# Second cross attention of a perceiver block: probabilities transposed in 32 by 32 blocks and moved by DMAs and copies, context in two buffers, and a planner with measured overlaps

## The chip, the cores and the metric

The kernel runs on one core of one Trainium2 chip. A core has a matrix engine (TensorE, "PE" in the profile), a vector engine (VectorE, "DVE"), a scalar engine (ScalarE, "ACT"), a general-purpose engine (GpSimd, "POOL") and a sync engine (SyncE, "SP") that here only issues DMAs. Each works through its own list of instructions in order and waits on semaphores for the others. Data lies in an on-chip memory with 128 partitions (rows); matrix products land in a separate accumulator memory of eight banks. All arithmetic is in 32-bit floats. The metric is the device time of one execution in microseconds (us), given as the median of several runs.

## The reference

There are 32 sequences of 64 tokens with 256 features (x), each with 256 context tokens of 256 features. Six layers follow one another, each added to x:

```
x = x + L0_xattn(ctx, layernorm(x))      # cross attention, 16 heads of 64, keys: context and latents
x = x + L0_attn(layernorm(x))            # linear attention, 16 heads of 16
x = x + L0_ffn(layernorm(x))             # gated feed-forward, hidden 768
x = x + L1_xattn(layernorm(x), ctx, ctx, mask)   # cross attention, 16 heads of 16
x = x + L1_attn(layernorm(x))            # recurrent layer (sLSTM), 64 units
x = x + L1_ffn(layernorm(x))             # 8 experts, entmax gates
```

The layer that the change is about is `L1_xattn`, standard cross attention: with q = x Wq + bq, k = ctx Wk + bk, v = ctx Wv + bv, split in 16 heads of 16,

```
p   = softmax(q k^T / 4 + mask)          # 64 queries by 256 context tokens, per head
out = (p v) Wo + bo
```

## The kernel before

The 2048 tokens are 16 tiles of 128 rows (two sequences each). The kernel has three parts that overlap at their seams:
- the first phase: `L0_xattn`, one sequence b after the other (32 of them);
- the second phase: the next three layers and the recurrent one, in 8 groups of two tiles (`linear_attention`, `feed_forward`, `queries`, then per tile `keys_values`, `scores`, `weighted`, `projected`, and `slstm_router` at the end of a group);
- the experts: gates, gathers of token rows, two matrix products per expert, and accumulating stores.

The order of the work is not the order of the program text. A planner (`Plan`) records every operation with what it reads and writes, a rank, and an estimated length (`PlanEngine.length`), and then lists all of them greedily: of the operations that are ready it takes the one that can start first by its own clock, ties by rank, at most 12 ranks ahead of the oldest operation left. So a change in an estimated length can reorder every engine's list. All recorded operations carry the line of the one helper that issues them (L375 in the profile), so the profile's groups are told apart by tile names. Tiles lie at fixed places of one large buffer, the arena (`ar.put(phase, tag, size, places)`); places may overlap those of an earlier part, and then wait for its last use. An operation written as `pl.copy` or `pl.either` may go to ACT or to DVE, as the planner finds.

In the first phase the softmax probabilities are transposed without PE: DVE transposes 32 by 32 blocks (`pl.vector.transpose` into tile `bT`), and 16 block moves put the blocks where they belong in `pT`: four on POOL, four on ACT or DVE, eight as DMAs on SP's queue. The planner takes 0.65 us to issue a DMA. 

In the second cross attention a run is one tile t with one half c of the heads, 32 runs in all. `scores` makes eight score products (tile `xsc`, four banks), masks each on DVE with its minimum (`tensor_tensor_reduce` into `xne` and `xnm`; a custom DVE operation in the profile), and takes the exponential on ACT into `xpr` with its sum into `xsm`. `weighted` then transposes the unnormalised probabilities on PE (16 transposes of 128 by 128 into the tile `xpTp`, four to a bank), copies each bank to `xpT`, transposes the reciprocal sums (`xrT`), multiplies values by the transposed probabilities (`xpo`), scales with the reciprocals and adds the two head halves and the value bias `vb` into `oT`. `projected` multiplies by `x_wo` (`xpw`) and adds to x.

Of the kernel before, what the change touches and what calls it, by code (L numbers as in the profile page):

```python
# [14 lines left out]
P = 128  # L15
# [139 lines left out]
class Slots:  # L155
# [7 lines left out]

    def take(self, t_):
        self.free.sort()
        self.next += 1
        return self.free.pop(0)
# [5 lines left out]
class Area:  # L173
# [9 lines left out]
    def room(self, t_, k):  # L183
# [3 lines left out]
        return all(a.next == len(a.asked) and a.live[j] is None for a, j in self.rivals[i])  # L187

# [21 lines left out]
class Plan:  # L210
# [10 lines left out]
    HOP = 0.06  # L221

    def __init__(self, tc):
        self.tc, self.ops, self.slots, self.news = tc, [], {}, []
        self.rank, self.group, self.lane, self.last = 0.0, None, None, {}
# [24 lines left out]
    @contextmanager  # L250
    def together(self, length):

        assert self.group is None
        self.group = []
        yield
        calls, self.group = self.group, None
        self.add({"PE": (length, calls)})
# [41 lines left out]
    def run(self, ahead):  # L299
# [7 lines left out]
        while todo:  # L307
# [3 lines left out]
            for op in sorted(ready, key=lambda op: op.rank):  # L311
# [5 lines left out]
                if op.news and not self.has_room(op):  # L317
                    if "PE" in op.ways and (short is None or op.rank < short.rank) and self.has_room(op, True):
                        short = op
                    continue  # L320
                for engine, (length, _) in op.ways.items():
                    at = free[engine]
                    for other in op.before:
                        at = max(at, other.end if other.on == engine and other.end == other.done else other.done + self.HOP)
                    for t_ in op.uses:
                        at = max(at, t_.free_at)
                    key = at, op.rank
# [9 lines left out]
            op.end = op.done = free[engine] = at + length  # L337
# [12 lines left out]
    def has_room(self, op, later=False):  # L350
# [10 lines left out]
        return True  # L361

# [76 lines left out]
class PlanEngine:  # L439
# [34 lines left out]
    def length(engine, name, args, kw):  # L474
# [10 lines left out]
        if name == "memset":  # L485
            return 0.1 + 0.5e-3 * n
        if engine == "ACT":
            if isinstance(kw.get("scale"), View):
                return 0.6
            return (0.12 + 0.91e-3 * n if name == "copy" else 0.33 + 0.66e-3 * n) + (0.19 if "accum_out" in kw else 0)  # L490
        if engine == "DVE":
            return 0.15 + 1.04e-3 * n + (0.08 if name == "tensor_tensor_reduce" else 0)
        if engine == "POOL":
            return 0.7 if n < 64 else 0.3 + 2.0e-3 * n
# [4 lines left out]
def kernel(ctx: ExitStack, tc: tile.TileContext, d: dict, out: bass.AP):  # L499
# [130 lines left out]
    with ExitStack() as sa:  # L630
# [21 lines left out]
        ar.put(1, "cx", 1024, 14336, 15360)  # L652
# [9 lines left out]
        for tag, size, *at in (  # L662
# [6 lines left out]
            ("ffh", 1536, 17920, 19456), ("sg", 512, 20992, 21504),  # L669
            ("xn0x", 256, 16384), ("xn1x", 256, 16640), ("xTx", 512, 16896, 17408), ("xq", 1024, 32256, 33280),  # L670
            ("xcT", 1024, 22016, 23040), ("xkT", 1024, 24064, 25088), ("xv", 1024, 30208, 31232),
            ("xpr", 2048, 26112, 28160), ("xpT", 512, 35328, 35840, 36352, 36864), ("xne", 256, 37376, 37632, 37888),
# [101 lines left out]
        def l0_context(t):  # L774

            pl.rank = 2 * t - 6.0
            cx = ar.tile([P, 4, D], F32, tag="cx", name=f"cx{t}")
            for b2 in range(2):
                b = 2 * t + b2
                pl.sync.dma_start(  # L780
                    out=cx[:, 2 * b2 : 2 * b2 + 2, :],
                    in_=d["ctx"][b * S2 : (b + 1) * S2, :].rearrange("(t p) d -> p t d", p=P),
# [14 lines left out]
            srcs = [cx[:, i, :] for i in range(4)]  # L797
            norm(srcs, srcs, f"c{t}", "c")
            affine(cx, 0, 4)
# [1134 lines left out]
```

## Time and profile before

| what | value |
|---|---|
| median of 3 runs | 1634.33 us (1632.51 to 1634.55) |
| profiled execution | 1633.02 us, its span 1631.3 us |
| mean granted clock of TensorE | 0.991 |
| instructions | 25951 |
| PE busy | 1579.4 us, 97% of the span |
| DVE busy | 1088.2 us, 67% |
| ACT busy | 693.8 us, 43% |
| POOL busy | 422.1 us, 26% |
| DMA | 95.02 MB, 58 GB/s over the span |

A span is the time from the first to the last instruction; the execution is a little longer. An engine's busy time counts each instant once, also where two of its instructions overlap, but the busy time of a group of instructions may overlap that of another group. Matmul instructions overlap their neighbours, and a matmul of 32-bit floats appears as two records. PEld is the loading of weights into the array, which runs beside the matmuls. Idle time of an engine is put down to the engine or transfer that ended it.

### The profile page before, as it was taken

How to read it: one execution, taken by the hardware profiler on the slowest of the kernel's cores; microseconds unless marked ns; L12 is line 12 of the kernel's file. 1: busy time of each engine (PE TensorE's matmuls, PEld its weight loads, DVE VectorE, ACT ScalarE, POOL GpSimd, SP SyncE). 2: the span in 40 equal slices, each digit the busy share in tenths (PEclk: the TensorE clock that was granted, in tenths of full speed). 3: DMA queues.
4: the chain of work that ended last, by engine and by line, in shares of the span. 5: the costliest groups of instructions: out<-in, count | busy, mean ns of one | idle time of the engine just before them, and what ended most of it. 6: DMA issues, size and time to landing. Idle time of an engine off the chain costs nothing. (4 is left out here: it accounts for less than half of the span.)

```text
span 1631.3 us, 25951 instructions
## 1 busy us (share of the span) xinstructions
PE 1579.4 (97%) x9226; PEld 1106.8 (68%) x9226; DVE 1088.2 (67%) x3089; ACT 693.8 (43%) x1813; POOL 422.1 (26%) x524
## 2 busy tenths in 40 slices
PE   8999999999999999999989999999999999999996
PEld 6556656565665656666556777777777776878885
DVE  6657666676766757776755788888888788762230
ACT  4434344353533535334421454454544547432332
POOL 5123123230333223331311221221212112223342
PEclk9999999999999999999999999999999999999998
DMA  6112112121112211122121000010000220455391
GB/s 212 38 30 59 38 31 44 38 59 29 39 30 46 47 34 40 30 71 53 38 54 49 14 27 27 18 37 14 27 27 20 85 80 19 133 144 141 69 307 31
DMA packets 95601, 95.02 MB, mean 58 GB/s; under 512 B 9327, under 2 KB 85936, under 8 KB 95472
## 3 DMA queue, kind: packets, MB, share of 16 engines
q1 hardware_dynamic: 89952, 85.41, 19.2%
q0 software_dynamic: 5520, 7.94, 2.4%
q8 instruction: 74, 1.21, 0.3%
q14 instruction: 55, 0.45, 0.1%
HBM read 63.63 MB, written 7.47 MB: 44 GB/s over the span
## 5 line engine op out<-in xcount | busy, mean ns | idle before, releaser
L375 PE MATMUL pu<-arena 128*128 128x512 f32 (+1 forms) x768 | 301.0, 615 | 3.5 <-ACT arena L375 2.8
L375 PE MATMUL sc<-arena 128*128 128x320 f32 x1024 | 290.5, 436 | 0.0
L375 PEld LDWEIGHTS sc<-arena 128*128 128x128 f32 x1024 | 190.8, 190 | 95.3 <-issue 19.2
L375 ACT ACTIVATE arena<-sc,nmax 128x320 f32<-128x320 f32 x256 | 134.4, 527 | 250.3 <-DVE nmax L375 241.8
L375 PEld LDWEIGHTS pu<-arena 128*128 128x128 f32 (+1 forms) x768 | 113.9, 189 | 175.9 <-issue 159.1
L375 POOL COPY arena<-arena 32x640 f32<-32x640 f32 (+1 forms) x161 | 108.9, 676 | 404.1 <-DVE arena L375 300.4
L375 DVE TENSOR_REDUCE nmax<-sc 128x1 f32<-128x320 f32 x256 | 121.8, 484 | 105.5 <-PE sc L375 104.1
L375 POOL TENSOR_TENSOR arena<-arena 128x1024 f32<-128x1024 f32 (+3 forms) x72 | 118.5, 1646 | 166.6 <-DVE arena L375 109.7
L375 ACT ACTIVATE arena<-arena,xnm 128x256 f32<-128x256 f32 x256 | 127.1, 500 | 52.1 <-DVE xnm L375 51.9
L375 DVE COPY arena<-pu 128x512 f32<-128x512 f32 x62 | 42.7, 689 | 115.4 <-PE pu L375 115.2
L375 DVE CUSTOM_DVE_ANT_0 arena<-xsc,arena 128x256 f32<-128x256 f32 x256 | 101.2, 421 | 17.7 <-ACT arena L375 10.3
L375 DVE TENSOR_TENSOR arena<-arena,sm 128x1280 f32<-128x1280 f32 x64 | 108.1, 1690 | 2.2
L375 DVE STREAM_TRANSPOSE arena<-arena 128x512 f32<-128x512 f32 (+1 forms) x192 | 104.4, 594 | 3.6
L375 ACT COPY arena<-pu 128x512 f32<-128x512 f32 x66 | 38.4, 585 | 128.0 <-PE pu L375 128.0
L375 POOL DMA_INDIRECT out<-arena x25 | 39.6, 1585 | 102.8 <-DVE arena L375 71.2
L375 PE MATMUL pqk<-arena 64*128 64x256 f32 x512 | 63.1, 383 | 1.6 <-ACT arena L375 1.6
L375 PE MATMUL xpTp<-ident,arena 128*128 128x128 f32 x512 | 63.6, 274 | 0.9 <-ACT arena L375 0.9
L375 PE MATMUL xak<-arena 128*128 128x512 f32 x128 | 62.3, 610 | 0.0
L375 PEld LDWEIGHTS xpTp<-ident,arena 128*128 128x128 f32 x512 | 56.9, 141 | 7.2 <-DVE arena L375 2.2
L375 PE MATMUL xav<-arena 128*128 128x256 f32 x256 | 61.5, 384 | 0.0
L375 PEld LDWEIGHTS po<-arena 128*64 128x64 f32 x1024 | 55.5, 137 | 8.8 <-issue 8.3
L375 PE MATMUL mepha<-arena 128*128 128x256 f32 x256 | 60.1, 385 | 1.4 <-ACT arena L375 1.4
(395 smaller groups left out, 2800.9 us busy)
## 6 DMA issues: line engine op xcount, KB each, us to landing
arena<-in_m_w SPq DMA_DIRECT2D x26, 1024.0 KB
arena<-arena SPq DMA_DIRECT2D x256, 80.0 KB
arena<-in_ctx SPq DMA_DIRECT2D x32, 256.0 KB
arena<-in_ctxT SPq DMA_DIRECT2D x16, 512.0 KB
x<-in_x SPq DMA_DIRECT2D x16, 128.0 KB
arena<-in_l0x_wkv SPq DMA_DIRECT2D x2, 1024.0 KB
arena<-arena SPq DMA_DIRECT2D x16, 128.0 KB
out<-x SPq DMA_DIRECT2D x16, 128.0 KB
```

Of the source, the lines that this page charges most:

```text
L375: r = getattr(real, name)(*[get(a) for a in args], **{k: get(a) for k, a in kw.items()})
```

## The change

The change has five parts.

First, the second cross attention no longer transposes on PE. DVE transposes the exponentials of each sequence of the run in 32 by 32 blocks (one instruction over 128 rows by 1024 columns, two per run) into a tile `xbT`, and 16 moves of 32 rows by 512 columns bring them to `xpT`: four on POOL, four on ACT, eight as DMAs of 64 KB on SP's queue. `xpr` now has three buffers of half the size; `xbT` and `xpT` have one each. A copy to POOL, to ACT or a DMA is chosen by a function `move`, which the first phase uses too.

Second, the value bias no longer enters each run. It is multiplied by `x_wo` once, ahead of the groups, and added to the row `x_bo`; the sum of the two head halves, now without the bias, goes to POOL. Four steps of the recurrent layer go from DVE to POOL in all groups but the last.

Third, the first phase's context tile `cx` is two tiles of one sequence each, so each is loaded, scaled and released by itself.

Fourth, the places in the arena change: the hidden layer of the feed-forward (`ffh`) has one buffer instead of two, and its second place now holds the second buffer of the context load `xcT`, which the second expert's weights will later overlie.

Fifth, the planner's estimates change: PE groups are taken 1.5% shorter, an engine is free again 0.085 us (DVE), 0.11 (ACT) or 0.05 (POOL) before its instruction ends, lengths for ACT, DVE and POOL are new, and the start of an operation counts when its buffer comes free.

```diff
+    def when(self, k):
+        return sorted(self.free)[k]
...
+    OVERLAP = {"DVE": 0.085, "ACT": 0.11, "POOL": 0.05}
...
-        self.add({"PE": (length, calls)})
+        self.add({"PE": (0.985 * length, calls)})
...
+                since = self.since(op)
                 for engine, (length, _) in op.ways.items():
-                    at = free[engine]
+                    at = max(free[engine], since)
                     for other in op.before:
-                        at = max(at, other.end if other.on == engine and other.end == other.done else other.done + self.HOP)
+                        at = max(at, other.done + (0.03 if other.on == engine else self.HOP))
...
-            op.end = op.done = free[engine] = at + length
+            op.end = op.done = at + length
+            free[engine] = op.end - self.OVERLAP.get(engine, 0.0)
...
-            return (0.12 + 0.91e-3 * n if name == "copy" else 0.33 + 0.66e-3 * n) + (0.19 if "accum_out" in kw else 0)
+            return (0.12 + 0.91e-3 * n if name == "copy" else min(0.33 + 0.66e-3 * n, 0.6)) + (0.09 if "accum_out" in kw else 0)
         if engine == "DVE":
-            return 0.15 + 1.04e-3 * n + (0.08 if name == "tensor_tensor_reduce" else 0)
+            return 0.15 + 1.04e-3 * n + (0.02 if name == "tensor_tensor_reduce" else 0)
         if engine == "POOL":
-            return 0.7 if n < 64 else 0.3 + 2.0e-3 * n
+            if n < 64:
+                return 0.7 if n <= 2 else 1.0
+            return 0.15 + 0.97e-3 * n if name == "tensor_copy" else 0.3 + 1.9e-3 * n
...
-        ar.put(1, "cx", 1024, 14336, 15360)
+        ar.put(1, "cx", 512, *range(14336, 16384, 512))
...
-            ("ffh", 1536, 17920, 19456), ("sg", 512, 20992, 21504),
+            ("ffh", 1536, 17920), ("sg", 512, 20992, 21504),
...
-            ("xcT", 1024, 22016, 23040), ("xkT", 1024, 24064, 25088), ("xv", 1024, 30208, 31232),
-            ("xpr", 2048, 26112, 28160), ("xpT", 512, 35328, 35840, 36352, 36864), ("xne", 256, 37376, 37632, 37888),
+            ("xcT", 1024, 22016, 19456), ("xkT", 1024, 23040, 24064), ("xv", 1024, 30208, 31232),
+            ("xpr", 1024, 25088, 26112, 27136), ("xbT", 2048, 28160), ("xpT", 2048, 35328), ("xne", 256, 37376, 37632, 37888),
...
+        def move(n, o, i, tight=False):
+            if n == 0:
+                pl.gpsimd.tensor_copy(o, i)
+            elif n == 1 and tight:
+                pl.scalar.copy(o, i)
+            elif n == 1:
+                pl.copy(o, i)
+            else:
+                pl.sync.dma_start(out=o, in_=i)
...
+        pl.vector.tensor_copy(vd, vb.unsqueeze(2).to_broadcast([P, 2, P]))
+        pvb = bank([P, D], "pvb")
+        with pl.together(0.9):
+            for c in range(2):
+                mm(pvb, vd[:, c], x_wo[:, c, :], start=(c == 0), stop=(c == 1))
+        pl.vector.tensor_tensor(row("x_bo"), pvb, row("x_bo"), ALU.add)
...
+            bT = ar.tile([P, 4, 2, 2, 4, B_], F32, tag="xbT", name=f"xbT{nm}")
+            for b2 in range(2):
+                pr = ar.tile([P, 4, S2], F32, tag="xpr", name=f"xpr{nm}_{b2}")
+                for j in range(4):
                     ne = ar.tile([P, S2], F32, tag="xne", name=f"xne{nm}_{j}_{b2}")
                     nmax = sp.tile([P, 1], F32, tag="xnm", name=f"xnm{nm}_{j}_{b2}")
                     pl.vector.tensor_tensor_reduce(ne, scs[j][:, b2, :], mb, 1.0, 3.0e38, ALU.add, ALU.min, nmax)
-                    pl.scalar.activation(
-                        pr[:, b2, j, :], ne, AF.Exp, bias=nmax, scale=-1.0, accum_out=sm[:, b2, j : j + 1]
+                    pl.scalar.activation(pr[:, j, :], ne, AF.Exp, bias=nmax, scale=-1.0, accum_out=sm[:, b2, j : j + 1])
+                pl.vector.transpose(
+                    bT[:, :, b2].rearrange("p k d j c -> p j d k c"),
+                    pr.rearrange("p j (d k c) -> p j d k c", d=2, c=B_),
+                )
+            pT = ar.tile([P, 4, 2, 2, 4, B_], F32, tag="xpT", name=f"xpT{nm}")
+            for n in range(4):
+                for a in range(4):
+                    k = (a + n) % 4
+                    move(
+                        n,
+                        pT[B_ * k : B_ * k + B_, a].rearrange("p b d j c -> p (b d j c)"),
+                        bT[B_ * a : B_ * a + B_, k].rearrange("p b d j c -> p (b d j c)"),
+                        tight=True,
                     )
...
-            pTs = {}
-            for b2 in range(2):
-                for kc in range(2):
-                    pT = ar.tile([P, 4, P], F32, tag="xpT", name=f"xpT{nm}_{b2}_{kc}")
-                    pT_ps = bank([P, 4, P], f"xpTp{nm}_{b2}_{kc}")
-                    with pl.together(T4):
-                        for j in range(4):
-                            tr(pT_ps[:, j, :], pr[:, b2, j, kc * P : (kc + 1) * P], ident)
-                    pl.copy(pT, pT_ps)
-                    pTs[b2, kc] = pT
...
-                                pTs[b2, kc][:, j, :],
+                                pT[:, :, b2, kc, j, :],
...
-            pl.vector.scalar_tensor_tensor(
-                oT[:, c], om[:, :, 0, :], vb[:, c : c + 1], om[:, :, 1, :], ALU.add, ALU.add
-            )
+            pl.gpsimd.tensor_tensor(oT[:, c], om[:, :, 0, :], om[:, :, 1, :], ALU.add)
...
-            pl.vector.tensor_scalar(il[:, :, :, 1:], il[:, :, :, 1:], 20.0, None, ALU.min)
+            side = pl.vector if g == NG - 1 else pl.gpsimd
+            side.tensor_scalar(il[:, :, :, 1:], il[:, :, :, 1:], 20.0, None, ALU.min)
...
-            pl.vector.tensor_tensor(tmp, m[:, :, 0:S], lf[:, :, 1:], ALU.add)
-            pl.vector.tensor_tensor(tmp, tmp, m[:, :, 1:], ALU.subtract)
+            side.tensor_tensor(tmp, m[:, :, 0:S], lf[:, :, 1:], ALU.add)
+            side.tensor_tensor(tmp, tmp, m[:, :, 1:], ALU.subtract)
...
-            pl.vector.tensor_tensor(iz[:, :, 1:], tmp2, z, ALU.mult)
+            side.tensor_tensor(iz[:, :, 1:], tmp2, z, ALU.mult)
```

## The prediction

> **What bounds the kernel now.** First I read the page's busy shares (columns: busy time, share of the span, instructions), then its 40 slices:
>
> ```profile
> PE 1579.4 (97%) x9226; PEld 1106.8 (68%) x9226; DVE 1088.2 (67%) x3089; ACT 693.8 (43%) x1813; POOL 422.1 (26%) x524
> ...
> PE   8999999999999999999989999999999999999996
> ...
> DVE  6657666676766757776755788888888788762230
> ```
>
> TensorE (PE) is full from end to end; VectorE (DVE) comes nearest in slices 23 to 34. That share is an average, so next the windows (length, then busy time and instructions of each engine, clock, DMA share, GB/s): the second phase's steady part, the first phase, the passage between them, the experts.
>
> ```profile
> 905.30:1364.80 459.50, 451.06 (x3454) 337.96 (x3453) 371.70 (x1365) 234.72 (x680) 86.01 (x160) 1.00 0.10 34
> 100.00:750.00 650.00, 647.80 (x3126) 409.20 (x3125) 441.87 (x857) 276.68 (x668) 182.19 (x182) 1.00 0.19 41
> 840.00:870.00 30.00, 24.13 (x150) 14.47 (x147) 21.92 (x68) 7.28 (x14) 9.28 (x16) 0.89 0.14 29
> 1400.00:1632.00 232.00, 209.20 (x1217) 182.29 (x1215) 78.47 (x355) 70.02 (x180) 75.32 (x67) 0.96 0.48 136
> ```
>
> PE idles 0.3% of the first phase and 8.4 of 459.5 us in the second: matmul time taken out of either shortens the run until another engine is late. The period of a group comes from the tile view of the query projection (count; shortest, median, longest; first and last start):
>
> ```profile
> L375 PE MATMUL xaq<-arena x64: 379/379/379, 905.3 to 1364.8; 128*128 128x256 f32 x64
> ```
>
> Eight groups start in it, so a group is (1364.8 - 905.3) / 7 = 65.6 us. By the window above it holds DVE 371.7 / 7 = 53.1 us (81%), ScalarE (ACT) 33.5, GpSimd (POOL) 12.3, and PE idle 1.2.
>
> **What is removed.** The groups by form (count | busy, mean ns of one | idle before, releasers):
>
> ```profile
> L375 PE MATMUL xpTp<-ident,arena 128*128 128x128 f32 x512 | 63.6, 274 | 0.9 <-ACT arena L375 0.9
> L375 DVE COPY arena<-xpTp 128x512 f32<-128x512 f32 x60 | 40.0, 685 | 4.5 <-PE xpTp L375 4.3
> L375 ACT COPY arena<-xpTp 128x512 f32<-128x512 f32 x68 | 38.6, 587 | 39.9 <-PE xpTp L375 39.8
> L375 DVE STREAM_TRANSPOSE arena<-arena 128x512 f32<-128x512 f32 x128 | 83.5, 690 | 3.6
> L375 DVE STREAM_TRANSPOSE arena<-arena 128x256 f32<-128x256 f32 x64 | 25.8, 402 | 0.0
> ```
>
> Matmuls overlap, so 63.6 us counts overlaps twice. What a transpose takes from the path is its pace, from PE's timeline (start, length, instruction):
>
> ```profile
> 921.70 1.91 PE L375 MATMUL xpTp<-ident,arena 128*128 128x128 f32 x16
> 923.45 0.38 PE L375 MATMUL xrT<-ident,arena 128*128 128x128 f32 x2
> ```
>
> (923.45 - 921.70) / 16 = 0.109 us; times 512 = **56.0 us** off PE, 7.0 per group. Ends of this term: 55 and 63.6.
>
> **What is added, and where it lies.** Per group of four runs (two token tiles by two channel halves), each run now having two DVE transposes of 128x1024 and 16 block moves of 32x512:
> - DVE: by the two transpose rows an element costs (690 - 402) / 256 = 1.125 ns, so 128x1024 is 690 + 512 x 1.125 = 1266 ns; 8 of them are 10.1. The instruction order of the changed kernel has, per group, fewer: 8 PSUM copies (5.5), 2 copies of xrT (0.8), 4 additions of oT now on POOL (1.4), 4 steps of the recurrent layer moved to POOL (1.3), one each of laq and xak (1.2); more: one copy of tr_me, one normalisation (1.1). Net +1.0: DVE 54.2 us.
> - ACT: 16 block copies; 32x640 took 722 ns, so 32x512 about 0.58: +9.2, less 8.5 x 0.587 = 5.0, plus about 1 taken over from DVE: 38.8.
> - POOL: 16 block copies at 0.61 (766 ns x 4/5) are 9.8, four oT additions 2.2, the recurrent steps about 2.4: 26.7. POOL's own order also carries the small powers of the layer norms behind block copies that wait for DVE.
> - SP: 8 DMAs of 64 KB per run; the first phase does the same with 80 KB.
>
> At PE's new period of 65.6 - 7.0 = 58.6 us DVE stands at 92%, ACT at 66%, POOL at 46%: all below PE, DVE barely. That cover pays for the added work; gone, each us of DVE is a us per group.
>
> **The new wait.** The context matmuls (xpo) wait for all 16 moves, and behind them on PE stands everything else. The moves wait on SP for DVE's transposes and, the target having one buffer, for the previous xpo; behind them on SP queue the next context load and, once a group, the stores of x. The delay is bounded by the first phase's last use of the same path (timelines of DVE, SP, PE):
>
> ```profile
> 845.87 1.63 DVE L375 STREAM_TRANSPOSE arena<-arena 128x512 f32<-128x512 f32 x3
> ...
> 847.20 5.16 SPq L375 DMA_DIRECT2D arena<-arena  x8
> ...
> 854.03 2.38 PE L375 MATMUL pu<-arena 128*128 128x512 f32 x5
> ```
>
> Eight issues take 5.2 us, and all had landed 6.8 us after the first. Softmax of a run (scores done 1064.3, last exponential done about 1069.0) takes 4.7 us when DVE does nothing else; in the order of the changed kernel about 2.2 us of other DVE work stands between (two additions to x, layer-norm statistics, a masked product). Scores to ready: 4.7 + 2.2 + 1.3 + 6.8 = 15.0 us at most. In the changed order PE has between a run's scores and its xpo, at the paces of the rows, 21 us for half of the runs and 13.9 for one of the short ones (projections of the feed-forward layer 5.2, keys and values 3.5, attention of the first kind 1.9, other scores 1.1, the rest 2.2). So a short run may wait 0 to 1.1 us: 16 x that is **0 to 18 us**. I take **5**, near the low end, since the first phase leaves 13.6 us between scores and context and PE lost nothing there:
>
> ```profile
> 506.67 1.34 PE L375 MATMUL sc<-arena 128*128 128x320 f32 x4
> ...
> 521.60 9.35 PE L375 MATMUL pu<-arena 128*128 128x512 f32 x24
> ```
>
> **Two rules against the change.** The Trainium skill, "VectorE: DVE Perf Modes", section "Rules for kernel authors", sends a 128x128 transpose to TensorE where PSUM will do as destination; by it the trade saves nothing, and the sum would stay at 1633. The rows say otherwise here, because PE, not DVE, is full. The Trainium skill, "DMA: Bandwidth & Descriptors", section "Anatomy of one DMA", gives a DMA about 2.0 us fixed plus its bytes over 436 GB/s; an estimate from it, were eight served one by one, is 17 us per run, 10 more than the trace's bound, and 16 short runs would make the sum about 1740. The trace's eight overlap.
>
> **The small edits.** The value bias folded into x_bo adds two matmul calls and one copy ahead of the loop: +0.9 (xpw's two calls pace 0.9). The second-phase chain gets longer by POOL's 555 ns in place of DVE's 329 (four times a group); PE's feed-forward and key work covers it, else 1 us per group. The layer-0 context in two tiles turns 32 POOL operations of 2526 ns into 64 of 1351, +5.6 us on an engine 28% busy there: 0, covered by PE's own work; uncovered it is those 5.6. One feed-forward buffer instead of two: its users are a group apart, 0. The second expert's weights now lie over the second context buffer and can load only after its last use; if that is late, 2 MB at the 236 to 369 GB/s of the first 20 us cost 6 to 9 us. The planner's new durations reorder all queues. Its reach is the idle time elsewhere: 11 us in the first 100, 5.9 at the passage (with the clock at 0.89), 22.8 at the end, 12 of them after the last matmul. I take 0 with ends of -15 and +10: in the first phase the changed order leaves about the same PE work between scores and context, and no row tells the sign.
>
> **The sum**, against the profiled execution (1633.0; span 1631.3): 1633.0 - 56.0 + 0.9 + 5 + 0 = 1582.9. The median shown is 1.3 higher: **1584 us**, 3.1% less.
>
> **Rivals.**
> 1. *DVE sets the pace* (0.20). For: 92% with in-order waits, where the fullest 100 us of the trace (1300 to 1400) had it at 83.7%. Against: its instructions start 0.08 us before the previous one ends when work is queued, so a denser stream needs less than its sum. At 88% a group takes 54.2 / 0.88 = 61.6: 4.0 x 8 = 32 saved, 1603 us; range 1597 to 1625.
> 2. *The new order also fills idle time* (0.10): 10 to 15 of the 40 us named above: 1570.
> 3. *SP holds the moves* (0.07, the slower side). Once a group two output stores stand in the queue before eight moves, and wait for DVE's last x; in the trace SP stood 224.5 us for that in 8 waits, the longest 46.5, with nothing urgent behind. Each us that x comes after the moves' inputs stops xpo and PE. Break-even is 55.1 / 8 = 6.9 us a group; at 10 us it is +25: 1659. Against: the stores are placed where their inputs are planned to be ready.
> 4. *The transposes were hidden* (0.03): DVE keeps most of its idle 12.5 us a group, and nothing comes of it: 1634. Against: PE's 1.2 us idle in a group.
>
> **How the numbers follow.** The forecast has 0.60 with 1569 to 1597 of its own. 0.2% (3 us) is about what this kernel's times can tell apart. Faster: 0.60 + 0.20 + 0.10 = 0.90; same 0.03; slower 0.07. The range 1562 to 1610 leaves out the slower rival, the unchanged one, the upper half of the first rival's, and some of the second's: about 0.2.
>
> **What the profile after should show.** No xpTp; start of the second phase unmoved (first xaq near 905); the group period 58.6 to 60; DVE at 90% or more there; PE's waits on DMA or DVE before xpo under 10 us; 64 DVE transposes near 1.27 us. A period of 61 or more with PE waiting for DVE is rival 1; SP waiting for DVE x with PE waiting for moves is rival 3. I am wrong if the idle time at the passage or in the experts moves by over 15 us.

## The result, and the profile after

The changed kernel takes 1658.6 us (median; 1657.0 to 1661.6), the kernel before 1633.9 in the same session: a ratio of 1.0155 with a 95% interval of 1.0137 to 1.0172. It is slower by 1.5%; the forecast was 1584, faster by 3%. The profiled execution took 1661.6 us, span 1659.8.

First the page of after, busy shares and three of the rows of 40 slices:

```profile
PE 1546.5 (93%) x8718; PEld 1066.8 (64%) x8718; DVE 1058.1 (64%) x3004; ACT 747.6 (45%) x1904; POOL 542.7 (33%) x744
...
PE   7999999999999999999989988989889798899996
...
DVE  7656666666666756667555688778787778643131
...
PEclk9999999999999999999989999999999896999998
```

PE's busy time fell by 33 us, not by the 55 of the forecast, and its idle time rose from 52 to 113. The digits say where: from slice 21 on, which is the passage and the second phase. The windows of after (columns as before: length, busy time of PE, PEld, DVE, ACT, POOL, then clock, DMA share, GB/s) put numbers on the second phase's steady part, the first phase, the passage and the experts:

```profile
909.00:1376.90 467.90, 417.92 (x2978) 299.74 (x2977) 361.09 (x1271) 275.53 (x736) 175.59 (x317) 0.95 0.22 59
100.00:750.00 650.00, 644.15 (x3107) 407.08 (x3107) 421.46 (x848) 276.31 (x673) 192.97 (x206) 1.00 0.19 40
840.00:870.00 30.00, 21.82 (x80) 10.71 (x76) 17.30 (x54) 6.02 (x13) 8.13 (x11) 0.83 0.13 27
```

The query projections mark the groups (first and last start):

```profile
L395 PE MATMUL xaq<-arena x64: 379/379/793, 909.0 to 1376.9; 128*128 128x256 f32 x64
```

So I divide the span in three: head (to the first query projection), seven groups, and end (from the last query projection). Before: 905.3, 459.5, 266.5. After: 909.0, 467.9, 282.9. The group went from 65.6 to 467.9 / 7 = 66.8 us, where the forecast had 58.6; PE idles 50.0 of the 467.9 us (8.4 before), and the clock granted in this stretch is 0.95 (1.00 before).

A seventh of this stretch is a rough measure of a group, because the planner puts work of the first group ahead of the first query projection and work of the last one behind the last. In before the first of the seven intervals is 53.4 us and the other six are 67.4 to 67.6. So the windows from the second to the seventh query projection, five whole groups, stand beside it; first before, then after:

```profile
958.68:1295.72 337.04, 332.11 (x2562) 248.02 (x2561) 275.39 (x991) 168.56 (x491) 67.05 (x128) 1.00 0.09 31
965.09:1303.85 338.76, 304.79 (x2241) 218.70 (x2240) 267.84 (x940) 201.00 (x540) 135.33 (x247) 0.96 0.23 62
```

By these "inner" groups PE has 512 records a group before and 448 after; a group took 337.04 / 5 = 67.4 us and takes 67.8, and the forecast's 7.0 less would be 60.4. Either way a group is some 7 to 8 us longer than forecast.

What PE waits for there (instruction, releaser; total, times, longest):

```profile
PE tr_ff L395 <- DVE arena L395: 8.0, 5, 2.0
PE xrT L395 <- POOL arena L395: 6.3, 12, 0.7
PE tr_la L395 <- ACT arena L395: 5.0, 5, 1.2
PE ffg L395 <- DVE xnm L395: 3.7, 1, 3.7
PE tr_xa L395 <- DVE arena L395: 3.2, 6, 1.2
PE xpo L395 <- ACT arena L395: 3.0, 2, 2.2
PE xpo L395 <- DVE xnm L395: 3.0, 2, 1.8
```

Many small waits, most of 0.5 to 2 us, on the layer norms (tr_...), on GpSimd (xrT) and ahead of the context matmuls, where the moves end (xpo). Summed over the whole view, 33.9 us end with VectorE, 9.1 with ScalarE, 6.3 with GpSimd and 0.6 with a DMA; 9.8 of all these stand before xpo. No single one explains the loss. PE's timeline at the end of one group (start, length, instruction, idle before):

```profile
1104.95 0.66 PE L395 MATMUL tr_la<-ident,arena 128*128 128x128 f32 x4 [1.17 <-ACT arena L395]
1107.10 1.09 PE L395 MATMUL tr_ff<-ident,arena 128*128 128x128 f32 x4 [1.49 <-DVE arena L395]
1108.11 2.09 PE L395 MATMUL xsc<-arena 32*128 32x256 f32 x16
1110.13 3.49 PE L395 MATMUL ffg<-arena 128*128 128x256 f32 x8
1113.45 1.89 PE L395 MATMUL laq<-arena 128*128 128x256 f32 x8
```

After two idles the scores take 2.09 us (1.15 elsewhere) and the first gate projection 3.49 (1.89 elsewhere): the clock is granted at half here. The trace records such a stretch of 6.8 us at this place in four groups running, and 92 us in all against 20 in before (each without the stretch that ends the trace).

The second thing to see lies on VectorE. Of its groups by form, in three steady groups of each kernel (count | busy, mean ns | idle), first before, then after:

```profile
L375 DVE SCALAR_TENSOR_TENSOR x<-arena,r_lay,x 128x256 f32<-128x256 f32 x6 | 2.6, 482 | 0.1
L375 DVE TENSOR_SCALAR arena<-x,mv_ff,r_ff 128x256 f32<-128x256 f32 x3 | 1.2, 409 | 0.0
L375 DVE SCALAR_TENSOR_TENSOR r_xa<-t_xa,r_xa 128x2 f32<-128x2 f32 x3 | 0.5, 153 | 0.0
```

```profile
L395 DVE SCALAR_TENSOR_TENSOR x<-arena,r_lay,x 128x256 f32<-128x256 f32 x6 | 5.7, 985 | 0.1
L395 DVE TENSOR_SCALAR arena<-x,mv_ff,r_ff 128x256 f32<-128x256 f32 x3 | 2.9, 966 | 0.0
L395 DVE SCALAR_TENSOR_TENSOR r_xa<-t_xa,r_xa 128x2 f32<-128x2 f32 x3 | 1.7, 566 | 0.0
```

The same instructions take two to four times as long. The timelines of DVE and of POOL at one such place:

```profile
1161.62 0.57 DVE L395 SCALAR_TENSOR_TENSOR r_xa<-t_xa,r_xa 128x2 f32<-128x2 f32 x1
1162.27 0.56 DVE L395 SCALAR_TENSOR_TENSOR nmr_xa<-mv_xa,r_xa 128x2 f32<-128x2 f32 x1
...
1166.27 1.89 DVE L395 SCALAR_TENSOR_TENSOR x<-arena,r_lay,x 128x256 f32<-128x256 f32 x2
```

```profile
1161.34 2.95 POOL L395 COPY arena<-arena 32x512 f32<-32x512 f32 x4 [3.75 <-DVE ve_lay L395]
...
1166.29 1.59 POOL L395 TENSOR_TENSOR x<-x,rows 128x256 f32<-128x256 f32 x2
```

Each long one lies beside a GpSimd instruction: the first two beside the block copies, the third beside an addition. Summed over the second phase (909 to 1377), the excess over the usual length of the same form is some 20 us in after (19.8 by my reckoning) and a few us in before (2.4; up to 7 by other choices of the usual length). Instructions that read PSUM, the accumulator memory, show none of it (the softmax's maximum is 0.41 us beside GpSimd and 0.41 alone), nor do the transposes (1.24 and 1.24), nor the layer norms' statistics, which read one operand of SBUF, the on-chip memory (0.43 and 0.41). The Trainium skill, "GPSIMD Engine Reference", section "Specifications", says that GpSimd's memory interfaces are shared with VectorE and contend with its instructions that have two SBUF inputs or run in a two-port mode: the rows with two SBUF inputs agree, and I had not looked for it. Of the tensor_scalar, which has one such input beside two pointers to scalars and is stretched too (409 to 966 ns), no run here shows the mode.

### The profile page after: what moved, and what is told of

It reads as the page before. It is cut to its first block, busy times and chain, and to the rows that moved or that the text cites. A ratio compares the mean times of both kernels' runs of the same rounds, so it can differ in the third digit from the quotient of the medians.

```text
span 1659.8 us, 25703 instructions
## 1 busy us (share of the span) xinstructions
PE 1546.5 (93%) x8718; PEld 1066.8 (64%) x8718; DVE 1058.1 (64%) x3004; ACT 747.6 (45%) x1904; POOL 542.7 (33%) x744
## 3 DMA queue, kind: packets, MB, share of 16 engines
q8 instruction: 70, 1.15, 0.3%
## 5 line engine op out<-in xcount | busy, mean ns | idle before, releaser
L395 POOL COPY arena<-arena 32x640 f32<-32x640 f32 (+2 forms) x289 | 204.0, 706 | 563.8 <-DVE arena L395 414.4
L395 PE MATMUL pu<-arena 128*128 128x512 f32 (+1 forms) x768 | 305.3, 615 | 4.5 <-DMA arena<-arena 2.9
L395 POOL TENSOR_TENSOR arena<-arena 128x512 f32<-128x512 f32 (+2 forms) x157 | 141.9, 923 | 162.3 <-DVE arena L395 123.2
L395 DVE STREAM_TRANSPOSE arena<-arena 128x512 f32<-128x512 f32 (+2 forms) x256 | 182.9, 753 | 6.5 <-ACT arena L395 4.7
L395 ACT COPY arena<-arena 32x512 f32<-32x512 f32 (+1 forms) x192 | 125.1, 651 | 58.2 <-DVE arena L395 46.9
L395 DVE TENSOR_TENSOR arena<-arena,sm 128x1280 f32<-128x1280 f32 x64 | 101.3, 1583 | 1.9
L395 POOL DMA_INDIRECT out<-arena x25 | 39.8, 1592 | 101.6 <-DVE arena L395 81.3
L395 PE MATMUL po<-arena 128*64 128x128 f32 x1024 | 61.3, 275 | 2.7 <-DVE arena L395 2.4
L395 PE MATMUL xav<-arena 128*128 128x256 f32 x256 | 63.8, 394 | 0.0
L395 PE MATMUL xak<-arena 128*128 128x512 f32 x128 | 62.4, 613 | 1.4 <-DVE x L395 1.4
L395 PE MATMUL pw<-arena 128*128 128x256 f32 x256 | 59.8, 386 | 0.0
```

The source lines that it names most:

```text
L395: r = getattr(real, name)(*[get(a) for a in args], **{k: get(a) for k, a in kw.items()})
```

## The experiments

The theories. **Moves:** xpo waits for the 16 moves. **GpSimd:** its new work stretches VectorE's instructions, and its own queue is later. **VectorE:** a backlog of its load in its in-order queue; over a steady group it is busy for 53.7 of 67 us, but unevenly, as the windows of its two halves show below. **Order:** the planner's new durations and overlaps give an order without slack. **Clock:** short idles set off half-clock stretches. All ratios are to the kernel before in the same session. "Period" is a seventh of the time from first to last query projection, "inner" the mean of the five intervals from the second to the seventh, "end" what follows the last, and "half clock" the time in us at half the clock, without the stretch that ends the trace. Where period and inner differ, the first or the last interval is short or long (over all runs single intervals go from 48.8 to 74.3 us), and inner is the better measure.

```profile
1139.00:1174.00 35.00, 30.79 (x228) 22.22 (x228) 31.71 (x127) 21.32 (x60) 14.30 (x22) 1.00 0.26 71
1104.00:1139.00 35.00, 31.16 (x225) 22.26 (x225) 23.93 (x73) 20.77 (x55) 13.73 (x29) 0.90 0.18 46
```

VectorE (the third busy time, behind PE and PEld) has 31.7 of 35 us in one half and 23.9 in the other, in which the clock is at 0.90.

| run | ratio (95% interval) | period | inner | end | half clock |
|---|---|---|---|---|---|
| before | 1 | 65.6 | 67.4 | 266.5 | 20 |
| after | 1.0155 (1.0137 to 1.0172) | 66.8 | 67.8 | 282.9 | 92 |
| old_planner | 1.0256 (1.0225 to 1.0287) | 63.9 | 66.1 | 299.7 | 130 |
| new_planner_alone | 1.0122 (1.0103 to 1.0140) | 67.6 | 69.7 | 263.6 | 10 |
| fill_pe | 1.0145 (1.0126 to 1.0164) | 65.4 | 65.8 | 280.8 | 61 |
| free_context | 1.0273 (1.0250 to 1.0296) | 65.4 | 66.0 | - | - |
| pool_cut | one run, 1631.0 us | 62.9 | 63.0 | - | - |
| moves_on_act | 1.0057 (1.0034 to 1.0079) | 63.1 | 66.0 | 288.9 | 51 |
| lean_to_act | 1.0027 (1.0014 to 1.0041) | 61.5 | 63.9 | 287.4 | 41 |
| half_blocks | 1.0048 (1.0034 to 1.0062) | 64.8 | 66.5 | 274.7 | 38 |
| planner_knows | 1.0065 (1.0039 to 1.0091) | 61.8 | 63.5 | 293.0 | 65 |
| both_reliefs | 0.9987 (0.9978 to 0.9997) | 61.9 | 63.8 | 281.4 | 41 |
| both_last_on_pe | 0.9987 (0.9973 to 1.0001) | 62.1 | 63.7 | 280.3 | 44 |
| reliefs_planner_knows | 1.0133 (1.0116 to 1.0150) | 63.2 | 64.7 | 295.2 | 68 |
| relief_side | 1.0008 (0.9995 to 1.0021) | 63.0 | 64.4 | 285.2 | 55 |
| relief_lean_more | 1.0028 (1.0016 to 1.0040) | 61.1 | 63.9 | 293.9 | 38 |
| relief_free_context | one run, 1652.7 us | 62.1 | 63.7 | - | - |
| relief_slack | 0.9948 (0.9928 to 0.9968) | 58.6 | 61.4 | 300.8 | 55 |
| after_slack | 1.0001 (0.9987 to 1.0015) | 62.4 | 62.3 | 284.4 | 79 |
| slack_last_on_pe | 0.9870 (0.9853 to 0.9886) | 59.3 | 62.0 | 286.5 | 41 |

One caution holds for most of them. Only free_context, fill_pe, pool_cut and relief_free_context keep the order of the kernel that they start from. In all others the planner makes a new order, and a new order alone can be worth 20 to 25 us (new_planner_alone below, and reliefs_planner_knows against both_reliefs), so in those runs the edit and the new order aren't parted.

### Body and planner apart

old_planner has the new body and the planner class of before; new_planner_alone the reverse.

> The changed kernel's body (transposes on VectorE, block moves, everything else) under the planner of before: its durations, no overlaps, no 0.985. If the planner's new, tighter durations are what lost the time (an order without slack, in which PE arrives at each result just before it is there), this takes 1585 to 1605 us, faster than before by 2 to 3%, and PE idles under 2.5 us a group. If the body itself loses (moves, longer chains through DVE and POOL), it stays at 1640 to 1670 with PE idle of 5 us or more a group.

> The body of before under the planner of after. If the planner's durations lose the time, PE idles more than the 52 us of before and the time rises to 1645 to 1660 us. If the body loses, it stays within 1620 to 1640.

Measured: each half alone is slower than before, by 2.6 and 1.2%. With the old body, the new planner's group is 67.6 us in place of 65.6 (inner 69.7 in place of 67.4), and VectorE's stretching some 15 us in place of a few: the new order alone sets VectorE's work beside GpSimd's. The new body under the old planner has a shorter group (63.9, inner 66.1), but loses 17 us in the head and 33 at the end. So neither theory of that pair holds alone: with the old body the new planner costs some 20 us by itself, and with the old planner the new body costs some 41.

### The moves and the clock, in after's own order

fill_pe (first edit) puts idle work ahead of two transposes; free_context (second) changes only what xpo reads:

```diff
+    FILL = ("tr_la", 10), ("tr_ff", 13)
...
+        if engine == "PE" and calls[0][0] == "transpose":
+            o, i, one = calls[0][1]
+            for tag, n in self.FILL:
+                if o.tile.name.startswith(tag) and o.tile.name[len(tag)].isdigit():
+                    for _ in range(n):
+                        self.tc.keep_in_program_order(real.transpose(o.real(), one, one))
```

```diff
+        held = [(t_, t_.ap) for t_ in op.uses if engine == "PE" and hasattr(t_, "stand")]
+        for t_, _ in held:
+            t_.ap = t_.stand
...
+            pT.tile.stand = arena[:, 0:2048].rearrange("p (a b c d e) -> p a b c d e", a=4, b=2, c=2, d=4, e=B_)
```

> After, in its own order, instruction for instruction; only the context matmuls (xpo) read a weight area of the same shape in place of the moved probabilities (this leaves the probabilities out of the context), so they no longer wait for the 16 moves, while all moves are still made. Waits before xpo in the second phase are some 16 us in after. If the latency of the moves is the cause of the lost time, directly and by what follows from it, the time falls by 30 us or more, to 1630 or less. If the chains through DVE, ACT and POOL ahead of the other PE work are, it falls by at most 16, to 1642 to 1655, and PE's waits before tr_la, tr_ff and xrT stay.

> After, in its own order, with 10 transposes of the identity put into PE's queue just ahead of tr_la and 13 ahead of tr_ff, once a group each, where PE idles 1.17 and 1.49 us in every steady group just before its clock is granted at half. They write where the true transposes write afterwards and change no result. Their own pace is 0.109 us, so 2.5 us a group, 20 us in all, against 2.7 us of idle. If short idles set off the half-clock stretches (92 us of them in after), those fall to below 60 us and the time by 8 to 20, to 1638 to 1650. If the clock follows something else, the half-clock time stays near 90 us and the time is that of after or up to 10 us longer.

free_context: first to last query projection, from its tile view:

```profile
L398 PE MATMUL xaq<-arena x64: 378/379/793, 909.6 to 1367.5; 128*128 128x256 f32 x64
```

457.9 us, 10.0 less than after, inner 66.0 in place of 67.8. The waits before tr_ff (8.0 us) and tr_la (5.0) are the same to the tenth. So the moves, with what follows from them, cost about 10 us of the 58 by which the seven groups exceed the forecast (467.9 - 7 x 58.6); that is also what stood before xpo (9.8). The rest of its time can't be compared: without the probabilities the tokens go to other experts (PE has 8772 records in place of 8718).

fill_pe, windows of after and of fill_pe over the same stretch of time, about three groups:

```profile
1036.38:1241.20 204.82, 184.40 (x1344) 132.28 (x1344) 161.43 (x569) 120.51 (x325) 81.31 (x147) 0.95 0.21 55
```

```profile
1036.38:1241.20 204.82, 192.76 (x1473) 141.29 (x1472) 168.78 (x589) 125.82 (x342) 82.98 (x150) 1.00 0.22 58
```

Identity transposes in the two idles, and the clock stays at 1.00: the four half-clock stretches of 6.8 us are gone. Two idles of 1.2 and 1.5 us, 3.3 us from the start of the first to the end of the second, had set them off. The Trainium skill, "TensorE: Matmul & The Clock Gate", section "Why this matters for your kernels", asks for no idle gap above some 3 us; here two shorter ones near each other did it. The groups became 10.1 us shorter, fillers included (inner 65.8 in place of 67.8), and the head 3.0 longer; the ratio, 1.0145 against 1.0155, can't be told from after's. PE still idles 34.1 us of the groups, beside the fillers' 2.8 us a group. So the half clock follows from what holds PE and adds 1.4 to 2.0 us to a group; the larger part of the 7 to 8 us is not the clock's.

### GpSimd's copies

pool_cut keeps every instruction and its place; GpSimd's copies only get short:

```diff
+        if engine == "POOL" and calls[0][0] == "tensor_copy" and calls[0][1][0].shape == [32, 512]:
+            calls = [("tensor_copy", tuple(v[:, 0:2] for v in calls[0][1]), {})]
```

> After, in its own order, instruction for instruction; only GpSimd's four block copies of a run copy 2 columns in place of 512 (this leaves three quarters... that is, the diagonal blocks of the probabilities, one in four, out of the context). What is read from it is the group period, 66.8 us in after (first to last query projection, 467.9 us over 7 groups). Theory 'shared work of POOL and DVE': VectorE instructions that run while GpSimd's copies run are stretched (19.8 us of such stretch in the second phase of after, 8.3 of them beside these copies, against 2.4 in before); then the stretch falls to about 11 us, and the period by 1.5 us or more, to 65.3 or less. Theory 'VectorE's own load': the period stays at 66.3 or above, since VectorE's instructions are all there.

Its query projections, and the three VectorE forms from above (three groups):

```profile
L398 PE MATMUL xaq<-arena x64: 379/379/635, 910.2 to 1350.4; 128*128 128x256 f32 x64
```

```profile
L398 DVE SCALAR_TENSOR_TENSOR x<-arena,r_lay,x 128x256 f32<-128x256 f32 x6 | 2.6, 482 | 0.1
L398 DVE TENSOR_SCALAR arena<-x,mv_ff,r_ff 128x256 f32<-128x256 f32 x3 | 2.9, 964 | 0.0
L398 DVE SCALAR_TENSOR_TENSOR r_xa<-t_xa,r_xa 128x2 f32<-128x2 f32 x3 | 1.7, 575 | 0.0
```

The period fell to 440.2 / 7 = 62.9, by 3.9 us (inner 63.0, by 4.8), with VectorE's and ScalarE's instructions all in place and in the same order. The excess went from 19.8 to 8.9 us, and PE's 6.3 us of waiting for GpSimd before xrT disappeared. Of the three forms x<-arena is back at 482 ns; in after it stood beside an addition of GpSimd, which now comes earlier. The other two stay long, beside other GpSimd instructions. This is the largest effect among the runs that keep after's order. How much of the 27 us is stretching (10.9 directly), how much GpSimd's shorter queue and how much the clock that came back with them (58 us at half in place of 92), this run doesn't part.

The same with all moves made, copies on ScalarE:

```diff
-            if n == 0:
+            if n == 0 and not tight:
                 pl.gpsimd.tensor_copy(o, i)
-            elif n == 1 and tight:
+            elif n < 2 and tight:
```

> The four block copies that GpSimd had in each run of the second cross attention go to ScalarE (8 of the 16 moves there, none on GpSimd), in a newly planned order. ScalarE rises from 39.4 to about 49 us of a group. If GpSimd's copies stretch VectorE on the path that sets the period, the time falls by 10 to 20 us, to 1635 to 1648. If VectorE's own load or the latency of the moves sets it, the time stays at 1650 to 1670.

1.0057, within the range that the theory of GpSimd gave. Its period of 63.1 says less than it seems to: the last interval is 54.4 us, and an inner group takes 66.0, 1.8 less than in after.

### VectorE's load

lean_to_act sets the planner's `lean` from 0.0 to 0.6; half_blocks transposes the first channel half on PE as before.

> The planner gives an operation that either engine can do to ScalarE, unless VectorE could start it 0.6 us sooner (in after: whichever starts sooner). By the planner's durations that takes 150 us off VectorE over the whole kernel and puts 155 on ScalarE. If VectorE's load sets the period of a group (53.7 of 67 us busy, without a gap from 1139 to 1174), the period falls by 3 us or more and the time to 1615 to 1635. If it is the latency of the moves, the stretching by GpSimd or the tight plan, the time stays at 1650 or above.

> The first channel half of each token tile has its probabilities transposed on TensorE again (as in before), the second by blocks and moves (as in after): PE gets 3.5 us a group back, VectorE gives 2.5, the moves are halved. If a chain through VectorE, GpSimd and the moves sets the period of after, that chain is cut and PE sets it again at about 62 us: 1600 to 1620 us in all, faster than both kernels. If the planner's order loses the time whatever the body is (as it did with the body of before), it is 1640 to 1655.

lean_to_act: VectorE's busy time falls from 1058 to 921 us, the period to 61.5 (inner 63.9), the ratio to 1.0027. So less load on VectorE helps about as much as shorter copies on GpSimd. half_blocks, expected below both kernels, has 64.8 (inner 66.5) and 1.0048: PE idles less (30.7 us of the seven groups), but half of the transposes are back on it, and it ends slower than before.

### Together

> The two edits that took most off the period, together: the four block copies of GpSimd on ScalarE, and the planner's preference for ScalarE (here 0.3 us). Periods measured so far: 66.8 us after, 63.1 with the copies moved, 61.5 with the preference of 0.6. If stretching by GpSimd and VectorE's load are separate costs, they add: a period of 60 us or less, the second phase 12 us or more shorter than with one of them, and 1615 to 1630 us in all. If both cure the same backlog, the period stays at 61 to 63 and the time at 1630 to 1645.

> As both_reliefs, and the last group (two token tiles, four runs) has its probabilities transposed on TensorE again, as before. From the last query projection to the end takes 266.5 us in before, 282.9 in after, 288.9 with the copies on ScalarE and 287.4 with the preference for it. If that tail is longer because no later group covers the moves of the last runs (and because gathers and expert weights share their queues), it falls to 272 or less here, and the time is 8 us or more below both_reliefs. If the tail is longer for other reasons (the planner's order, the expert weights loading later), it stays at 280 or more.

> The body of after, planned by durations that hold what the runs showed: a VectorE instruction that reads SBUF alone is planned to start only when the GpSimd instruction in flight has ended, and the issue of a block move by DMA is planned at 0.75 us in place of 0.65. Everything else is as in after. If what was lost in after is the difference between the plan and the chip at these two places, the time falls to 1625 to 1645. If not, it stays at 1650 or above.

> both_reliefs planned with the same two corrections as planner_knows. If the corrections matter beside the two reliefs, it is 5 us or more below both_reliefs, at 1605 to 1625; if the reliefs already took the cause away, it lies within 5 us of it.

both_reliefs (copies on ScalarE and lean 0.3) has a period of 61.9, inner 63.8, and 0.9987: the two reliefs don't add, as would be so if both cure the same backlog. planner_knows all but removes the stretching by order alone (excess 1.9 us) and gets 61.8 (inner 63.5), again some 4 to 5 us, but loses 10 at the end. With the reliefs its corrections hurt (1.0133); neither expectation had this, and I can't explain it. And the last group on PE changed nothing there (end 280.3 against 281.4): PE's idle time fell by 8.7 us, the transposes cost 7.

### What was still open

> both_reliefs with the steps of the recurrent layer that the change gave to GpSimd back on VectorE, and the two matmuls of the folded value bias (pvb) due only just before their result is needed. In both_reliefs PE waits 7.7 us before slp, 7.0 before xrT (for GpSimd) and 2.2 before pvb. If those waits come from GpSimd's longer chain, 6 to 12 us go: 1612 to 1621. If VectorE is what is late, it stays at 1622 to 1632.

> both_reliefs in its own order, with xpo reading a weight area in place of the moved probabilities (this leaves the probabilities out of the context), so that PE never waits for a move. Read from it is the period of a group, 61.9 us in both_reliefs. If the latency of the moves still holds PE, the period falls to 60 or less. If not, it stays within 0.7 us.

relief_side gains nothing (1.0008): the recurrent layer's steps on GpSimd and the place of pvb, undone together, are not what holds PE. relief_free_context has a period of 62.1 against 61.9 (inner 63.7 against 63.8): with the reliefs the moves' latency holds PE no longer within the groups.

relief_slack is one line on top of both_reliefs:

```diff
-    OVERLAP = {"DVE": 0.085, "ACT": 0.11, "POOL": 0.05}
+    OVERLAP = {}
```

> both_reliefs planned without the overlaps of the new planner (a queue's next instruction is planned at the end of the previous one, as in before's planner). By its durations the plan is 27 us longer, so it leaves slack on VectorE and ScalarE. If the order of after is too tight for the chip, this is faster: 1610 to 1622. If the overlaps are right and the order is not what holds PE, it is 1630 to 1645.

> relief_side with a preference of 0.6 us for ScalarE in place of 0.3 (65 us less on VectorE, 68 more on ScalarE by the planner's durations). If VectorE's load still sets the pace, it is 5 us or more below relief_side; if ScalarE has become as full as VectorE was, it is the same or slower.

> After with one line changed: the planner's overlaps are left out, as in relief_slack; GpSimd keeps its copies and the planner its preferences. If the tight order is what lost most of the time, the period falls to 61 or less and the time to 1625 to 1640. If GpSimd's stretching and VectorE's load are, whatever the slack, the period stays at 63 or more and the time at 1645 or above.

> relief_slack with the last group's probabilities transposed on TensorE. If the uncovered moves of the last group make the end long, it falls from 300.8 us by 10 or more and the time to 1605 to 1615, the fastest of all. If the end is long for the chain of the experts' routing on VectorE and the half clock that follows it, it stays within 6 us of 300.8 and the time within 5 of relief_slack.

Query projections, their window, and the window of the five inner groups in relief_slack:

```profile
L395 PE MATMUL xaq<-arena x64: 379/379/483, 911.9 to 1322.2; 128*128 128x256 f32 x64
```

```profile
911.90:1322.20 410.30, 389.65 (x2937) 282.89 (x2936) 329.35 (x1170) 340.16 (x861) 105.58 (x205) 1.00 0.24 65
964.19:1271.26 307.07, 292.32 (x2209) 211.41 (x2209) 249.57 (x902) 257.11 (x650) 83.86 (x164) 1.00 0.25 66
```

410.3 / 7 = 58.6 us. That this is the forecast's period to the tenth is chance: the last interval is 49.4 us (69.9 in after), and the stretch holds 2937 records, where before's 3454 less 7 x 64 transposes are 3006, so some of the work has moved out of it. An inner group takes 307.07 / 5 = 61.4 us, 1.0 above the 60.4 of the forecast (with 442 records in place of 448, so rather 2), and the clock is at 1.00; PE idles 20.7 us from first to last in place of 50.0. So with the reliefs and more room in the plan the group comes near the forecast. The same line alone, in after, gives 62.4 (inner 62.3) and takes 1.5% off: the kernel is then as fast as before (1.0001). More lean (relief_lean_more, 1.0028) doesn't help: in an inner group of 63.9 us ScalarE is then busy for 52.8 and VectorE for 50.0.

relief_slack loses most of it at its end (300.8), in small part because work of its last group lies there (1544 records, 1514 in after). What a last group looks like in after: the queues of SP and of POOL ahead of the last xpo, which waits 5.9 us:

```profile
1435.47 5.33 SPq L395 DMA_DIRECT2D arena<-in_m_w  x3
1440.88 2.37 SPq L395 DMA_DIRECT2D arena<-in_m_b  x1
1443.34 10.12 SPq L395 DMA_DIRECT2D arena<-arena  x8
```

```profile
1445.99 0.97 POOL L395 DMA_INDIRECT arena<-xd,arena  x1 [0.30 <-issue]
1446.96 0.62 POOL L395 COPY arena<-arena 32x512 f32<-32x512 f32 x1
1452.89 1.91 POOL L395 COPY arena<-arena 32x512 f32<-32x512 f32 x3 [5.30 <-DMA arena<-xd,arena]
```

The eight issues stand behind expert weights and take 10.1 us (5 to 6 in a steady group), half of it one gap after the sixth; what made the gap, no run shows. GpSimd's copies stand behind a gather. With the last group's transposes on PE (slack_last_on_pe) the end falls from 300.8 to 286.5 and the kernel takes 1613.2 us: **0.9870 (0.9853 to 0.9886), the fastest, ahead of both kernels.** That the edit did nothing without the slack fits an end that other waits then held; which ones wasn't tried.

## Why the prediction was wrong, point by point

- *56.0 us off PE, 7.0 a group:* right. At full clock, in relief_slack, PE is busy for 58.5 us of an inner group in place of 66.4; its five groups hold 32 records fewer than five times 448, which is part of the difference. *The group of 65.6 us* that it was taken from was read too low: a steady group of before is 67.4, so the forecast for one is 60.4, not 58.6. relief_slack takes 61.4 with somewhat less work in it.
- *The costs of the added work:* right. Transposes of 128x1024 take 1239 ns (1266 forecast), copies 616 on ScalarE and 629 on GpSimd (580, 610); of a steady 67 us VectorE has 53.7 (54.2), ScalarE 39.8 (38.8), GpSimd 26.5 (26.7).
- *"All below PE, DVE barely. That cover pays for the added work":* this is the step that failed. A share below 100% was taken for cover. VectorE is busy for 361.1 of the 467.9 us, 77%, and yet PE idles 50.0, 33.9 of them until VectorE by the trace. VectorE's work is not spread: from 1139 to 1174 it idles 3.3 us of 35, and PE waits 2.6 for it there; before that, at 1111, it stands 4.2 us for PE (laq). Rival 1 (0.20) named the engine, but priced it by share, at 61.6 us a group; the group took 66.8.
- *GpSimd at 26.7 us, below PE, at no cost:* an omission inside the same step. Cutting its copies is worth 3.9 us a group, 27 us over seven. The trace of before had the clue in a few us of stretched instructions, the page cited above had the rule; doubled work on GpSimd should have been priced by what it does to VectorE.
- *The reorder term, 0 with ends of -15 and +10:* mis-sized beyond its ends. The new planner alone costs the old body 1.2%, some 20 us; one line of slack takes 25 us from after. Which of the planner's other edits cost how much wasn't tried.
- *The wait of xpo, 5 us of 0 to 18:* about 10 in the groups, plus 5.9 at the last run: 16, within its ends, three times my value. The 2.0 us for a DMA that the prediction set against this term belongs, where it is cited, to DMAs that GpSimd issues; these moves are issued by SP.
- *Clock:* not priced. 72 us more at half clock than before; PE's busy time therefore fell by 33 us instead of 55. It follows from the idle time and comes on top of it.
- *The end, taken as unchanged:* 16 us longer. The prediction looked at what covers the moves in a group, not in the last one, where the experts' weights and gathers share the queues.
- *Small terms:* pvb cost 0.9 as forecast and another 1.3 of waiting for x_wo. In the first phase PE is busy for 644.2 of 650 us (647.8 before), a loss of 3.6. It is the new order more than the split context: new_planner_alone, which has the old context, has 643.5, and old_planner, which has the split one, 646.6. So the split cost about 1 us, where I had 0.
- *Rival 3, SP holds the moves at the stores of x:* not seen in the groups: SP waits for x there, but the moves behind start as the second transpose ends (1079.28 and 1079.21 us). The slower side, at 0.07, came by a mechanism that I had not named.

The account: against 1576 us (the span before, less 55 of PE work) the span of 1660 has 61 us more idle time (8 in the head, 42 in seven groups, 11 at the end) and 22 us more PE busy time, the matmuls at the lower clock.

Not settled: the effects of GpSimd, of VectorE's load and of the slack overlap (each alone some 4 to 5 us a group, together 6 to 8), so no share of the loss belongs to one of them; nor why the old planner does worse with the new body; and how much of any newly planned run is luck of its order.

## What to carry to other kernels

When work is taken from a full engine in a statically ordered kernel, the next bound is not the next share: find the stretch in which the second engine has hardly a gap, and ask who waits at its end. Work given to GpSimd lengthened VectorE's instructions on SBUF operands beside it here (482 to 985 ns), so price it on VectorE's path. A plan can be too tight: leaving out overlaps that the trace truly shows made this kernel 1.5% faster, and both_reliefs 0.4%. But longer durations are no rule: the old planner, without overlaps and with longer durations on GpSimd, was the slowest with this body (1.0256). And measure a period between points that hold the same work: first to last start hid 2 to 3 us of a group here.

## What the hardware showed that I had not expected

- VectorE instructions with only SBUF operands took up to some 0.5 us longer beside a GpSimd instruction (482 to 985 ns, 153 to 566 ns), but not all of them: those that read PSUM, the 32x32 transposes and the layer norms' statistics took no longer.
- Two PE idles of 1.2 and 1.5 us within 3.3 us brought 6.8 us of half clock, in four groups running; with 23 identity transposes in their place those stretches did not come.
- Issues of eight 64 KB block moves took 5 to 6 us in the steady groups, and 6.7 to 10.1 in the last three runs, where weight loads share the queue.
